# A bidirectional scan kernel: the neighbour chunk's state as an extra column of the data, and sums of a layer's last chunk from an accumulator

## The chip, the cores and the metric

One core of one Trainium2 chip. The metric is device microseconds of the whole kernel; the median of three runs before the change is 5370.0 us (5369.94 to 5373.72).

## What is computed

The input is 16 images of 192 channels and 56 x 56 = 3136 positions. Three layers of one kind and one of another follow each other, each adding to x what it computes from a group norm of x.

A layer of the first kind (RWKV's WKV, in both directions) makes k, v and r by 192 x 192 products, and runs along the 3136 positions, forward and backward, with a fixed decay per channel:

```python
no = jnp.maximum(o, u + kt)
A = jnp.exp(o - no)
Bw = jnp.exp(u + kt - no)
y = (A * p + Bw * vt) / (A * q + Bw)
```

The state p is a decayed sum of exp(k) v, q one of exp(k). The mean of the forward and the backward y is multiplied by sigmoid(r), normalised over the channels, multiplied by Wo and added to x. The last layer takes the maximum of x at neighbours two rows and two columns away (cyclic), concatenates x and that maximum less x, and applies a 1 x 1 convolution, batch norm and GELU.

## The kernel before

Two images are one pair: 2 x 192 channels are three rows (`j`) of 128 partitions, rows 0 and 2 the first 128 channels of either image, row 1 the other 64 of both. A pair's 3136 positions are 7 chunks of L = 448. There are 8 pairs, in two streams of four. Each pair goes through the runs of three WKV layers and one convolution layer; between layers its chunks lie in DRAM.

**Slots.** All chunk-sized data live in 33 slots of SBUF, `Slot` (L501). A slot holds three rows of L + 2 columns; `t` is columns 0 to L - 1, `full` all of them. Column L of an x chunk takes the group mean (`mean_column`, L750), so that the products deliver their own bias. Slots are handed out first in, first out.

**A forward unit (A)** of a chunk: keys (`a_keys`, `a_exp`: ek = exp(k)), values (`a_values`; for the last chunk it also writes the mean column, since the gate product will read it), q scan over ek (`a_q`), `a_save`, bonus (`a_den`), inversion by Ln and Exp on ScalarE, ekv = v ek (`a_ekv`), p scan over ekv (`a_p`), its `save`, bonus (`a_num`), product on POOL (`a_y`).

**A backward unit (B)** runs from the last chunk to the first: gate (`b_gate`, `b_exp`), q and p scans in reverse (`b_q`, `b_p`), `b_den`, `b_num`, mixing on POOL (`b_mix`), squares and their channel sums (`b_squares`, `b_sums`), deviation (`b_rs1` to `b_rs3`), spreading it by TensorE (`b_spread`), `b_scale`, output product (`b_out`), residual (`b_x`), statistics for the next layer's group norm (`b_stats`, by `chunk_stats` on ScalarE). **A convolution unit (C)** is `c_rows`, `c_columns`, `c_product`, `c_end`; beside its chunk it loads a ring, the two strips of the neighbour chunks, by two DMAs on SP (L813, L814).

**The scan** (L836) is one VectorE instruction per row. The decay comes from PSUM, the state of the neighbour chunk by `save` (L841): a copy of the last column of the three rows into a small carry tile, which the scan takes as its initial value. The q carry is copied on ScalarE, the p carry on POOL or VectorE. The first chunk of a direction has the constant 0.0.

**The bonus** (L849) is one VectorE instruction on rows 0 and 2 and one on row 1, in place.

**The order** on every engine is written out by hand. Steps pair a B unit of one stream with an A or C unit of the other. There are 102 steps with B and A (`both_a`, `both_a_first`), 42 with B and C (`both_c`), 66 with A alone (`forward_a`), 14 with C alone (`forward_c`), 24 with B alone (`backward_alone`). After a layer's B chunk 0 the other stream's last A unit runs alone: there `forward_a` holds the late parts `l` of that B chunk, from `b_rs2` to `b_x` and the statistics. With the sums complete, `norm_sums` (L728), `norm_var` and `norm_fold` make the next layer's norm; `gap()` places one of these parts where one is pending.

The waits between instructions are not written by hand. They are put in when the program is built, from the stretches of the tiles that each instruction reads and writes.

```python
self.full = keep.tile([P, 3, L + 2], F32, tag=self.tag, name=name(what))
self.t = self.full[:, :, 0:L]
...
init = 0.0 if first else run.carry[key][:, j, :]
V.tensor_tensor_scan(
    s.t[:, j, order], dec[:, column(j)].to_broadcast([P, L]), data.t[:, j, order], init, ALU.mult, ALU.add
)
```

Of the kernel before, what the change touches and what calls it, by code (L numbers as in the profile page):

```python
# [473 lines left out]
def fast_path(ctx: ExitStack, tc: tile.TileContext, flag, x, wproj, wfold, wcfold, wconst, wgroup, sums, picks, vecs, out):  # L474
# [26 lines left out]
    class Slot:  # L501
        def __init__(self, what):
            self.tag = free.pop(0)
            self.full = keep.tile([P, 3, L + 2], F32, tag=self.tag, name=name(what))
            self.t = self.full[:, :, 0:L]
# [25 lines left out]
    def column(j):  # L531
        return slice(j % 2, j % 2 + 1)
# [172 lines left out]
    class Run:  # L705
        def __init__(self, pr, l, stats, src=None, first=None):
            self.pr, self.l, self.stats, self.src = pr, l, stats, src
            self.xa, self.xb, self.xz = {}, {}, {}
            if first is not None:
                self.xa[0] = first  # L710
            self.begun = False
            self.bias, self.carry, self.ps = {}, {}, {}
            self.ek, self.ekv, self.h, self.den, self.sg, self.rs = {}, {}, {}, {}, {}, {}
            self.m, self.ml, self.q, self.p = {}, {}, {}, {}
# [3 lines left out]

    def chunk_stats(stats, xt, c):

        for j in ORDER:
            S.activation(junk, xt[:, j, :], AF.Identity, accum_out=stats[:, 0, j, c : c + 1])  # L722
            S.activation(junk, xt[:, j, :], AF.Square, accum_out=stats[:, 1, j, c : c + 1])  # L723
# [106 lines left out]

    def scan(run, key, data, order, first, last):
        dec = params[run.l][0]
        s = Slot(key)
        for j in ORDER:
            init = 0.0 if first else run.carry[key][:, j, :]
            V.tensor_tensor_scan(  # L836
                s.t[:, j, order], dec[:, column(j)].to_broadcast([P, L]), data.t[:, j, order], init, ALU.mult, ALU.add
            )
        return s

    def save(run, key, s, col, eng=G):  # L841

        run.carry[key] = stile("c" + key)
        if key == "q":
            S.activation(run.carry[key], s.t[:, :, col : col + 1], AF.Copy)  # L845
        else:
            eng.tensor_copy(run.carry[key], s.t[:, :, col : col + 1])  # L847

# [4 lines left out]

    AHEAD, BACK = slice(0, L, 1), slice(None, None, -1)


    def a_keys(run, c):
        product(run, "k", run.w[0], run.xa[c], c == 0)
        run.ek[c] = Slot("ek")
        if c == 0:  # L860
            take_bias(run, "k", S)
# [17 lines left out]
    def a_ekv(run, c):  # L879
        if c == 0:  # L880
            take_bias(run, "v", V)
        e, ps, b = Slot("ekv"), run.ps["v"], run.bias["v"]
        run.ekv[c] = e
        for j in ORDER:
            V.scalar_tensor_tensor(e.t[:, j, :], ps[j][:, 0:L], b[:, j, :], run.ek[c].t[:, j, :], ALU.add, ALU.mult)  # L885
            release(ps[j])

    def a_q(run, c):
        run.den[c] = scan(run, "q", run.ek[c], AHEAD, c == 0, c == NL - 1)

    def a_save(run, c):
        save(run, "q", run.den[c], L - 1)

    def a_p(run, c, eng=G):
        run.h[c] = scan(run, "p", run.ekv[c], AHEAD, c == 0, c == NL - 1)
        if c < NL - 1:
            save(run, "p", run.h[c], L - 1, eng)

# [12 lines left out]
    def a_y(run, c):  # L911
# [3 lines left out]
        if c in (0, NL - 1):  # L915
# [4 lines left out]
            if c == NL - 1:  # L920
                G.tensor_mul(chk[:, 0], run.carry["q"], grow)

# [21 lines left out]
    def b_q(run, c):  # L944
        if c not in run.q:
            run.q[c] = scan(run, "q", run.ek[c], BACK, c == NL - 1, c == 0)
            if c > 0:
                save(run, "q", run.q[c], 0)

# [5 lines left out]
    def b_p(run, c):  # L955
        if c not in run.p:
            run.p[c] = scan(run, "p", run.ekv[c], BACK, c == NL - 1, c == 0)
            if c > 0:
                save(run, "p", run.p[c], 0)

# [62 lines left out]
    def b_x(run, c):  # L1023
        wob, ps, xs = params[run.l][4], run.ps["o"], run.xb[c]
        for j in ORDER:
            xj = xs.t[:, j, :]
            V.scalar_tensor_tensor(xj, ps[j][:, 0:L], wob[:, column(j)], xj, ALU.add, ALU.add)  # L1027
            release(ps[j])
        nc.sync.dma_start(run.dst[c], xs.t)

    def b_stats(run, c):
        xs = run.xb.pop(c)
        chunk_stats(run.new, xs.t, c)
        if c == 0:
# [331 lines left out]
    def forward_a(a, nback, nfront):  # L1366
# [10 lines left out]
        if l and late[l] == 0:  # L1377
            squares_and_sums(l)
            b_rs1(*l)
            late[l] = 0.5  # L1380
        if l and late[l] == 0.5:
            b_rs2(*l)
            b_rs3(*l)
            late[l] = 1
        if l:
            b_spread(*l)
        elif ahead:
            keys(nfront)
        store()
        a_q(*a)  # L1390
        a_save(*a)
        if ahead and not l:
            exp_keys(nfront)
        a_den(*a)
        gap()
        invert(den())
        a_ekv(*a)
        gap()
        if l:
            b_scale(*l)  # L1400
            if ahead:
                keys(nfront)
                exp_keys(nfront)
            b_out(*l)
            late[l] = 2
        sum_up()
        if nback is not None:
            b_gate(*nback[1:])
        a_p(*a)
        gap()  # L1410
        if l:
            add(l)
            sum_up()
        a_num(*a)
        a_y(*a)
# [237 lines left out]
```

## Time and profile before

| | |
|---|---|
| median of the runs | 5370.0 us |
| profiled execution | 5382.8 us |
| its span | 5381.0 us |
| VectorE busy | 5014.9 us (93%) |
| TensorE busy | 4629.7 us (86%) |
| ScalarE busy | 3681.2 us (68%) |
| GpSimd (POOL) busy | 2770.3 us (51%) |
| mean granted TensorE clock | 0.916 |

A row of the groups names the line, the engine, the operation, what it writes and reads, partitions x elements, and the count; then the busy time and the mean length of one, then the engine's idle time ahead of them and what ended most of it. Lengths of neighbours on VectorE overlap by some 0.08 us, so that a mean length is a little above busy time over count. In a timeline a row is a start, a length, engine, line and tiles; equal neighbours are merged (x3). DVE is VectorE, ACT ScalarE, PE TensorE, SPq the queue that issues most DMAs.

### The profile page before, as it was taken

Reading aid. Unit: us, or ns where it says so; the run is one execution under the profiler, and the core shown is the slowest. Engines: PE = TensorE matmul, PEld = TensorE weight load, DVE = VectorE, ACT = ScalarE, POOL = GpSimd, SP = SyncE. Lnnn points to the kernel's source line nnn. Section 1 sums busy time; section 2 is a strip of 40 time slices with the busy share of each in tenths; the row PEclk is TensorE's granted clock in tenths of the full one; section 3 lists DMA queues with packets and bytes.
Section 4 is the critical chain, followed back from the end, with each engine's and each line's share of the span. In section 5 each row is a group of like instructions: output and inputs, shape, how many; then the busy total and the mean of one; then the engine's idle time right before and its main releaser. Section 6 shows DMA issues by size and latency. Waiting matters only on the chain. (4 is left out here: it accounts for less than half of the span.)

```text
span 5381.0 us, 50984 instructions
## 1 busy us (share of the span) xinstructions
PE 4629.7 (86%) x15206; PEld 1498.6 (28%) x15206; DVE 5014.9 (93%) x6556; ACT 3681.2 (68%) x7035; POOL 2770.3 (51%) x2164
## 2 busy tenths in 40 slices
PE   6888988989798898888979888888888988898897
PEld 2222322223232222222323222222222222222222
DVE  6989999999999999999999999999999999999996
ACT  6777667767676676676667767667667566676673
POOL 1555555645454465555444455555535455555463
PEclk8989989989899898998989989999898998999898
DMA  5222212124243212213425121221343312222233
GB/s 149 78 80 72 85 66 88 63 90 140 87 131 89 82 63 73 74 67 105 144 87 150 56 74 67 85 74 62 111 139 94 111 56 74 70 77 80 77 102 115
DMA packets 314271, 482.42 MB, mean 90 GB/s; under 512 B 66432, under 2 KB 306688, under 8 KB 313984
## 3 DMA queue, kind: packets, MB, share of 16 engines
q1 hardware_dynamic: 312832, 477.59, 27.9%
q8 instruction: 123, 2.02, 0.2%
q10 hardware_dynamic: 1152, 1.48, 0.1%
q14 instruction: 164, 1.34, 0.1%
HBM read 324.83 MB, written 154.14 MB: 89 GB/s over the span
## 5 line engine op out<-in xcount | busy, mean ns | idle before, releaser
L913 POOL TENSOR_TENSOR p<-p,q 128x1344 f32<-128x1344 f32 x168 | 510.1, 3037 | 887.8 <-ACT q L909 472.1
L969 POOL TENSOR_TENSOR ekv<-ekv,ek 128x448 f32<-128x448 f32 x504 | 618.2, 1227 | 677.1 <-DVE p L1014 304.9
L836 DVE TENSOR_TENSOR_SCAN p<-fdecays,cp,ekv 128x448 f32<-128x448 f32 x864 | 928.5, 1130 | 7.2 <-POOL p L913 4.5
L836 DVE TENSOR_TENSOR_SCAN q<-fdecays,cq,ek 128x448 f32<-128x448 f32 x864 | 929.2, 1131 | 1.9 <-PE st L987 0.2
L971 POOL TENSOR_TENSOR p<-p,sg 128x448 f32<-128x448 f32 x504 | 599.4, 1189 | 54.5 <-ACT cq L845 10.7
L970 POOL TENSOR_TENSOR p<-p,ekv 128x448 f32<-128x448 f32 x504 | 600.6, 1192 | 39.5
L847 POOL COPY cp<-p 128x3 f32<-128x3 f32 x271 | 196.4, 725 | 686.9 <-DVE p L836 454.3
L978 ACT ACTIVATE ek<-p 128x448 f32<-128x448 f32 x504 | 283.6, 573 | 259.4 <-POOL p L971 257.5
L591 PE MATMUL ops<-p,fwo 128*128 128x448 f32 x336 | 223.5, 755 | 275.3 <-DVE p L1014 275.2
L866 ACT ACTIVATE ek<-k,k 128x448 f32<-128x448 f32 x504 | 292.1, 630 | 243.0 <-PE k L594 216.4
L723 ACT ACTIVATE fjunk<-x 128x448 f32<-128x448 f32 x672 | 387.6, 577 | 21.1
L722 ACT ACTIVATE fjunk<-x 128x448 f32<-128x448 f32 x672 | 384.6, 572 | 14.6
L851 DVE SCALAR_TENSOR_TENSOR q<-ek,fcc,q 128x896 f32<-128x896 f32 x336 | 337.1, 1043 | 51.1 <-ACT cq L845 51.1
L1009 PE MATMUL rsb<-rs,fpicks 32*128 32x448 f32 (+1 forms) x1008 | 335.8, 594 | 48.8 <-ACT rs L1003 46.7
L1027 DVE SCALAR_TENSOR_TENSOR x<-ops,fwob,x 128x448 f32<-128x448 f32 x504 | 315.9, 674 | 52.2 <-PE ops L594 27.1
L851 DVE SCALAR_TENSOR_TENSOR ek<-ek,fcc,q 128x896 f32<-128x896 f32 x336 | 361.6, 1117 | 2.8 <-POOL chk L919 2.8
L851 DVE SCALAR_TENSOR_TENSOR ekv<-ekv,fcc,p 128x896 f32<-128x896 f32 x336 | 330.4, 1024 | 1.2
L934 ACT ACTIVATE sg<-r,r 128x448 f32<-128x448 f32 x504 | 311.9, 624 | 15.8 <-PE r L594 10.4
L885 DVE SCALAR_TENSOR_TENSOR ekv<-v,v,ek 128x448 f32<-128x448 f32 x504 | 312.9, 677 | 0.0
L1014 DVE TENSOR_TENSOR p<-p,rsb 128x448 f32<-128x448 f32 x504 | 281.5, 614 | 31.1 <-PE rsb L1009 31.0
L851 DVE SCALAR_TENSOR_TENSOR p<-ekv,fcc,p 128x896 f32<-128x896 f32 x336 | 293.4, 913 | 10.0 <-POOL cp L847 9.7
L906 ACT ACTIVATE q<-q 128x1344 f32<-128x1344 f32 x168 | 222.4, 1324 | 90.4 <-DVE q L851 65.9
(232 smaller groups left out, 11795.3 us busy)
## 6 DMA issues: line engine op xcount, KB each, us to landing
x<-xd SPq DMA_DIRECT2D x240, 672.0 KB, 5.5
xd<-x SPq DMA_DIRECT2D x168, 672.0 KB, 4.0
x<-in_x_dram SPq DMA_DIRECT2D x320, 224.0 KB, 4.6
x<-in_x_dram SPq DMA_DIRECT2D x320, 112.0 KB, 4.6
out_dram<-ml SPq DMA_DIRECT2D x112, 224.0 KB, 2.3
ring<-xd SPq DMA_DIRECT2D x112, 168.0 KB, 5.3
wkv<-in_wfold_dram SPq DMA_DIRECT2D x24, 640.0 KB, 5.5
out_dram<-ml SPq DMA_DIRECT2D x112, 112.0 KB, 2.3
```

The source lines that it names most:

```text
L722: S.activation(junk, xt[:, j, :], AF.Identity, accum_out=stats[:, 0, j, c : c + 1])
L723: S.activation(junk, xt[:, j, :], AF.Square, accum_out=stats[:, 1, j, c : c + 1])
L836: V.tensor_tensor_scan(s.t[:, j, order], dec[:, column(j)].to_broadcast([P, L]), data.t[:, j, order], init, ALU.mult, ALU.add)
L851: by_channel(lambda js, i: V.scalar_tensor_tensor(dst.t[:, js, :], e.t[:, js, :], cc[:, i : i + 1], state.t[:, js, :], ALU.mult, ALU.add))
L885: V.scalar_tensor_tensor(e.t[:, j, :], ps[j][:, 0:L], b[:, j, :], run.ek[c].t[:, j, :], ALU.add, ALU.mult)
L913: G.tensor_mul(run.h[c].t, run.h[c].t, den.t)
L934: S.activation(sg.t[:, j, :], ps[j][:, 0:L], AF.Exp, bias=b[:, j, :], scale=-1.0, accum_out=run.chk[:, at : at + 1])
L969: G.tensor_mul(y.t[:, j, :], y.t[:, j, :], den.t[:, j, :])
L970: G.tensor_add(h.t[:, j, :], h.t[:, j, :], y.t[:, j, :])
L971: G.tensor_mul(h.t[:, j, :], h.t[:, j, :], sg.t[:, j, :])
L1009: PE.matmul(ps[j][:, :L], pick[rows, j, :], rs[rows, :], start=True, stop=True)
L1027: V.scalar_tensor_tensor(xj, ps[j][:, 0:L], wob[:, column(j)], xj, ALU.add, ALU.add)
```

## The change

A slot becomes one flat stretch of 3 (L + 2) + 2 columns, seen as three rows. `full` begins at column 2 of it; `lead` begins one column earlier, so that it has a column ahead of column 0. `save` copies the last state into the neighbour chunk's data: forward into the column ahead of the next chunk's ek or ekv, backward into column L of the previous chunk's. A scan that isn't a direction's first runs over L + 1 columns from the constant 0.0, and reads the state as its first element. For this the next chunk's ek and ekv slots are taken at the save if they don't exist yet (`slot_of`). The q save stays on ScalarE.

The residual of chunk 0, a layer's last, writes its row sums by an accumulator output of VectorE; ScalarE then forms only the squares of that chunk.

`forward_a` with late parts gets an order of its own: the q scan ahead of `b_rs2`, the output product ahead of the gate and of the keys, the bonus `a_num` ahead of the residual, and no `gap()`.

```diff
-            self.full = keep.tile([P, 3, L + 2], F32, tag=self.tag, name=name(what))
+            flat = keep.tile([P, 3 * (L + 2) + 2], F32, tag=self.tag, name=name(what))
+            rows = lambda at: flat[:, at : at + 3 * (L + 2)].rearrange("p (j n) -> p j n", j=3)[:, :, 0 : L + 1]
+            self.full, self.lead = rows(2), rows(1)
             self.t = self.full[:, :, 0:L]
...
-    def chunk_stats(stats, xt, c):
+    def chunk_stats(stats, xt, c, whole=False):
         for j in ORDER:
-            S.activation(junk, xt[:, j, :], AF.Identity, accum_out=stats[:, 0, j, c : c + 1])
+            if not whole:
+                S.activation(junk, xt[:, j, :], AF.Identity, accum_out=stats[:, 0, j, c : c + 1])
             S.activation(junk, xt[:, j, :], AF.Square, accum_out=stats[:, 1, j, c : c + 1])
...
-    def scan(run, key, data, order, first, last):
+    def scan(run, key, data, step, first):
         dec = params[run.l][0]
         s = Slot(key)
         for j in ORDER:
-            init = 0.0 if first else run.carry[key][:, j, :]
+            if first:
+                out, e = s.t[:, j, ::step], data.t[:, j, ::step]
+            elif step > 0:
+                out, e = s.lead[:, j, :], data.lead[:, j, :]
+            else:
+                out, e = s.full[:, j, ::-1], data.full[:, j, ::-1]
             V.tensor_tensor_scan(
-                s.t[:, j, order], dec[:, column(j)].to_broadcast([P, L]), data.t[:, j, order], init, ALU.mult, ALU.add
+                out, dec[:, column(j)].to_broadcast([P, L if first else L + 1]), e, 0.0, ALU.mult, ALU.add
             )
         return s
-    def save(run, key, s, col, eng=G):
-        run.carry[key] = stile("c" + key)
-        if key == "q":
-            S.activation(run.carry[key], s.t[:, :, col : col + 1], AF.Copy)
+    def save(s, step, to, eng=G):
+        src, dst = (s.t[:, :, L - 1 : L], to.lead[:, :, 0:1]) if step > 0 else (s.t[:, :, 0:1], to.full[:, :, L : L + 1])
+        if eng is S:
+            S.activation(dst, src, AF.Copy)
         else:
-            eng.tensor_copy(run.carry[key], s.t[:, :, col : col + 1])
+            eng.tensor_copy(dst, src)
...
+    def slot_of(slots, c, what):
+        if c not in slots:
+            slots[c] = Slot(what)
+        return slots[c]
...
     def a_p(run, c, eng=G):
-        run.h[c] = scan(run, "p", run.ekv[c], AHEAD, c == 0, c == NL - 1)
+        run.h[c] = scan(run, "p", run.ekv[c], AHEAD, c == 0)
         if c < NL - 1:
-            save(run, "p", run.h[c], L - 1, eng)
+            save(run.h[c], AHEAD, slot_of(run.ekv, c + 1, "ekv"), eng)
...
-            V.scalar_tensor_tensor(xj, ps[j][:, 0:L], wob[:, column(j)], xj, ALU.add, ALU.add)
+            V.scalar_tensor_tensor(
+                xj, ps[j][:, 0:L], wob[:, column(j)], xj, ALU.add, ALU.add,
+                accum_out=run.new[:, 0, j, c : c + 1] if c == 0 else None,
+            )
...
         xs = run.xb.pop(c)
-        chunk_stats(run.new, xs.t, c)
+        chunk_stats(run.new, xs.t, c, c == 0)
...
         if l:
+            if late[l] == 0.5:
+                b_rs2(*l)
+                b_rs3(*l)
+            b_spread(*l)
+            a_den(*a)
+            invert(den())
+            sum_up()
+            a_ekv(*a)
             b_scale(*l)
+            b_out(*l)
+            if nback is not None:
+                b_gate(*nback[1:])
             if ahead:
                 keys(nfront)
                 exp_keys(nfront)
-            b_out(*l)
-            late[l] = 2
...
+            a_p(*a)
+            a_num(*a)
             add(l)
             sum_up()
-        a_num(*a)
```

More of the change, by code (lines that the diff above doesn't have):

```diff
@@ L711, in __init__ @@
             self.begun = False
-            self.bias, self.carry, self.ps = {}, {}, {}
+            self.bias, self.ps = {}, {}
             self.ek, self.ekv, self.h, self.den, self.sg, self.rs = {}, {}, {}, {}, {}, {}
@@ L852, in bonus @@
             dst.t[:, js, :], e.t[:, js, :], cc[:, i : i + 1], state.t[:, js, :], ALU.mult, ALU.add))
-    AHEAD, BACK = slice(0, L, 1), slice(None, None, -1)
+    AHEAD, BACK = 1, -1
+    def slot_of(slots, c, what):
+        if c not in slots:
+            slots[c] = Slot(what)
+        return slots[c]
     def a_keys(run, c):
         product(run, "k", run.w[0], run.xa[c], c == 0)
-        run.ek[c] = Slot("ek")
+        slot_of(run.ek, c, "ek")
         if c == 0:
@@ L881, in a_ekv @@
             take_bias(run, "v", V)
-        e, ps, b = Slot("ekv"), run.ps["v"], run.bias["v"]
-        run.ekv[c] = e
+        e, ps, b = slot_of(run.ekv, c, "ekv"), run.ps["v"], run.bias["v"]
         for j in ORDER:
@@ L888, in a_q @@
     def a_q(run, c):
-        run.den[c] = scan(run, "q", run.ek[c], AHEAD, c == 0, c == NL - 1)
+        run.den[c] = scan(run, "q", run.ek[c], AHEAD, c == 0)
     def a_save(run, c):
-        save(run, "q", run.den[c], L - 1)
+        if c < NL - 1:
+            save(run.den[c], AHEAD, slot_of(run.ek, c + 1, "ek"), S)
+        else:
+            run.last = stile("cq")
+            S.activation(run.last, run.den[c].t[:, :, L - 1 : L], AF.Copy)
     def a_p(run, c, eng=G):
-        run.h[c] = scan(run, "p", run.ekv[c], AHEAD, c == 0, c == NL - 1)
+        run.h[c] = scan(run, "p", run.ekv[c], AHEAD, c == 0)
         if c < NL - 1:
-            save(run, "p", run.h[c], L - 1, eng)
+            save(run.h[c], AHEAD, slot_of(run.ekv, c + 1, "ekv"), eng)
     def a_den(run, c):
@@ L920, in a_y @@
             if c == NL - 1:
-                G.tensor_mul(chk[:, 0], run.carry["q"], grow)
+                G.tensor_mul(chk[:, 0], run.last, grow)
     def b_gate(run, c):
@@ L945, in b_q @@
         if c not in run.q:
-            run.q[c] = scan(run, "q", run.ek[c], BACK, c == NL - 1, c == 0)
+            run.q[c] = scan(run, "q", run.ek[c], BACK, c == NL - 1)
             if c > 0:
-                save(run, "q", run.q[c], 0)
+                save(run.q[c], BACK, run.ek[c - 1], S)
     def b_den(run, c):
@@ L956, in b_p @@
         if c not in run.p:
-            run.p[c] = scan(run, "p", run.ekv[c], BACK, c == NL - 1, c == 0)
+            run.p[c] = scan(run, "p", run.ekv[c], BACK, c == NL - 1)
             if c > 0:
-                save(run, "p", run.p[c], 0)
+                save(run.p[c], BACK, run.ekv[c - 1])
     def b_num(run, c):
@@ L1380, in forward_a @@
             late[l] = 0.5
[L1381 to L1387, printed above, removed]
+        if not l and ahead:
             keys(nfront)
@@ L1391, in forward_a @@
         a_save(*a)
[L1392 to L1398, printed above, removed]
-        if l:
+        if l:
+            if late[l] == 0.5:
[6 more added lines that the diff above has]
+            a_ekv(*a)
             b_scale(*l)
+            b_out(*l)
+            if nback is not None:
+                b_gate(*nback[1:])
             if ahead:
@@ L1403, in forward_a @@
                 exp_keys(nfront)
-            b_out(*l)
-            late[l] = 2
[L1406 to L1411, printed above, removed]
+            a_p(*a)
+            a_num(*a)
             add(l)
             sum_up()
-        a_num(*a)
+        else:
+            if ahead:
+                exp_keys(nfront)
+            a_den(*a)
+            gap()
+            invert(den())
+            a_ekv(*a)
+            gap()
+            sum_up()
+            if nback is not None:
+                b_gate(*nback[1:])
+            a_p(*a)
+            gap()
+            a_num(*a)
         a_y(*a)
```

## The prediction

> **What bounds the kernel now.** I read the page's busy shares first, then the groups by line with shapes kept apart, then the timeline of a layer end, then that of the tail.
>
> ```profile
> PE 4629.7 (86%) x15206; PEld 1498.6 (28%) x15206; DVE 5014.9 (93%) x6556; ACT 3681.2 (68%) x7035; POOL 2770.3 (51%) x2164
> ...
> L836 DVE TENSOR_TENSOR_SCAN q<-fdecays,cq,ek 128x448 f32<-128x448 f32 x864 | 929.2, 1131 | 1.9 <-PE st L987 0.2
> L836 DVE TENSOR_TENSOR_SCAN p<-fdecays,cp,ekv 128x448 f32<-128x448 f32 x864 | 928.5, 1130 | 7.2 <-POOL p L913 4.5
> ...
> L836 DVE TENSOR_TENSOR_SCAN q<-fdecays,ek 128x448 f32<-128x448 f32 x144 | 146.3, 1071 | 6.7 <-ACT ek L866 6.0
> L836 DVE TENSOR_TENSOR_SCAN p<-fdecays,ekv 128x448 f32<-128x448 f32 x144 | 146.1, 1070 | 0.0
> ```
>
> VectorE is the bound: 5014.9 of 5381.0 us, in order, and inside the paired steps it has almost no idle time. So microseconds of VectorE are microseconds of the kernel, except where it waits. The last two rows are the form that the change gives to all scans: no carry operand, initial value 0.0. It costs 1071 ns against 1131 ns.
>
> The largest repeated wait is at a layer end: VectorE's timeline, then ScalarE's and TensorE's in the same place (start, length, engine, line, idle time before).
>
> ```profile
> 2045.73 0.15 DVE L751 COPY x<-nm 128x3 f32<-128x3 f32 x1
> 2045.92 0.63 DVE L997 TENSOR_TENSOR rs<-st,rs 64x448 f32<-64x448 f32 x1
> 2046.58 3.23 DVE L836 TENSOR_TENSOR_SCAN q<-fdecays,cq,ek 128x448 f32<-128x448 f32 x3
> 2050.08 2.18 DVE L851 SCALAR_TENSOR_TENSOR q<-ek,fcc,q 128x896 f32<-128x896 f32 x2 [0.27 <-ACT cq L845]
> ...
> 2070.00 0.20 DVE L728 TENSOR_REDUCE mv<-stats 128x6 f32<-128x42 f32 x1 [3.17 <-ACT fjunk L723]
> ...
> 2065.80 0.58 ACT L722 ACTIVATE fjunk<-x 128x448 f32<-128x448 f32 x1
> ...
> 2048.22 0.54 PE L599 MATMUL v<-x,wkv 128*64 128x448 f32 x1
> ```
>
> The reduction L728 waits 3.17 us for six statistics that ScalarE works off from 2065.80 to 2069.97, 0.70 us each. There are 17 such ends; the row of L728 has 77.5 us of waits, 20.6 of it the start's. The last line matters below: the value product of that step ends on TensorE at 2048.76, 3 us after L751 has run.
>
> The tail is VectorE and SP, one convolution chunk after another:
>
> ```profile
> 5294.48 0.50 DVE L1051 TENSOR_TENSOR m<-ring,x 128x336 f32<-128x336 f32 x1
> 5294.89 0.85 DVE L1052 TENSOR_TENSOR m<-x 128x672 f32<-128x672 f32 x1
> ...
> 5298.22 1.56 DVE L1066 TENSOR_TENSOR ml<-ml,x 128x1344 f32<-128x1344 f32 x1
> 5299.81 1.56 DVE L1067 TENSOR_TENSOR m<-m,ml 128x1344 f32<-128x1344 f32 x1
> ...
> 5335.01 1.61 DVE L1051 TENSOR_TENSOR m<-ring,x 128x336 f32<-128x336 f32 x1 [2.58 <-DMA ring<-xd]
> ...
> 5330.25 0.59 SPq L813 DMA_DIRECT2D ring<-xd  x1
> 5330.88 0.62 SPq L814 DMA_DIRECT2D ring<-xd  x1
> ```
>
> L1052 needs nothing of L1051 and starts 0.09 us before its end. L1067 reads what L1066 writes and starts 0.03 us after its end. A VectorE instruction that must wait for the one just before it therefore costs 0.12 us more (117 ns in the trace's records: L1066 and L1067 start 34 ns after, unbound neighbours 83 ns before the end).
>
> [...]
>
> **The change part by part.**
>
> *Scans.* 1728 (864 + 864) lose 60 ns and gain one column: 1728 x 0.058 = -100 us. The carries are copied by the same engines at the same places. A group of three (0.17 us) gives nothing where VectorE then waits for TensorE anyway: L1027 waits 73 times, L1014 31, several of them in one step. For some 45 lost groups: +8.
>
> *What the flat tile does to the waits.* A slot was a three-dimensional tile; now it is a flat one, seen through a rearranged view. I built the changed program and compared the waits that it writes with those before. An access to rows 0 and 2 is now ordered against row 1, and a column of all three rows against the rows. The diff names none of this.
>
> (a) Each bonus is two instructions, rows 0 and 2, then row 1. The second now waits for the first: 4 x 168 = 672. With some that now wait for the scan just ahead, 708 bonus instructions wait for their predecessor; before, none. So do L1052 and L1053: 112. 820 x 0.117 = +96 us, less 4 for those inside waits that remain. On ScalarE 138 exponentials wait for the save just ahead; it is idle a third of the time, so nothing.
>
> (b) L751 (mean_column in a_values) writes column L of a chunk whose columns 0 to L-1 the value product is reading. It now waits for the product's last matmul. In the timeline above that is from 2045.73 to 2048.8, and over the 17 layer ends 3.0 to 4.1 us, mean 3.5. Behind it on VectorE stand the scan q, L997, the bonus, ekv and L1014, whose result TensorE needs for the output product, and behind that the gate product and the statistics.
>
> (c) A ring has two DMAs into disjoint columns (L813, L814). The second now waits for the first to land, about 4 us, and SP's later loads and stores stand behind it. In the paired steps the rings land over 20 us early, so nothing. In the tail three chunks have no margin (L1051 at 5335, 5344 and 5354): 3 x 4 = +12.
>
> *Earlier slots.* The next chunk's ekv slot is taken at the save, one step early. Every last user had finished over 2 us before the save's present place, so the saves wait for nothing new. Loads behind L971 wait 1.5 us on SP, far ahead of need. In the first forward and backward pass slots are short: three q scans would stand 3.7 to 6.3 us behind the POOL product L913, where p scans now stand 2.5 and 2.0. Bounds 0 and +16; I take +8.
>
> *Layer ends.* Three of six statistics go: 3 x 0.70 = -2.1 us on the path that ends at L728. The three others still start when TensorE's gate product has given ScalarE its bias, as now. L997 behind the scan removes the 0.27 us wait and, with the shorter scan, saves 0.5. So one end moves by 3.5 - 0.5 - 2.1 = +0.9; 17 of them +15. L1027's waits there (0.56, 0.59) are covered by the bonus put ahead, but the chain through TensorE is longer, so this gains nothing.
>
> *Accumulators.* 72 L1027 write a sum. Unknown: 0 to 0.6 us each (nothing, or the instruction again). 51 are covered by the wait at L728, which otherwise would lengthen VectorE's path by up to 1.8 us per end; I take +1, and up to +13.
>
> *The other order in forward_a.* In six ends beside a convolution the output product goes ahead of the keys and L1027 no longer waits 2.2 us. But there ScalarE's 18 statistics end the wait (2.91 us before the bonus); three are gone, and the exponential of the keys comes 2 us later in their place. Nothing.
>
> Sum: -100 + 8 + 96 - 4 + 12 + 8 + 15 + 1 = +36 us on the profiled execution (5382.8, span 5381.0). It lies 12.8 above the median of the runs, 5370.0; I add the same 36: 5406 us.
>
> **Rivals.** *The layer end wins, faster.* Place: L751 against the value product. If TensorE is through with that product when L751 comes, the 3.5 us go and each end gains about 2.6: 36 - 17 x 3.5 = -24, 5346 us. The sum changes sign where the wait is below 1.4 us. For: TensorE ran ops at half pace at 2054, so a shift could land in a better stretch of its clock. Against: the product follows the norm's sums on TensorE, and these follow POOL, which the change does not hasten.
>
> *The waits cost nothing.* Then it is the diff as it reads: -100 + 8 - 2.1 x 17 = 5242. Against: L1066 and L1067, each 56 times.
>
> *All cancels.* The waits at the ends fall half as long, and the tail's DMAs overlap otherwise: 5365 to 5380.
>
> *SP becomes the bound.* The ring's stall at each of 56 chunks pushes stores, and these free slots: 1 us at half the steps is 120 us, 5490. Against: over 20 us of margin.
>
> **How the numbers follow.** The forecast has 0.60, the layer end's rival 0.12, nothing-costs 0.05, all-cancels 0.17, SP 0.06. 0.2% is about what can be told from no change here, 11 us: faster 0.16, same 0.19, slower 0.65. The forecast's own range is 5383 to 5445: ends +-1 us (17), start 8, accumulators 12, lost overlap 10. To hold 8 in 10 it takes in all-cancels and the edge of the first rival: 5354 to 5450.
>
> **What would show it.** Scans at 1073 ns. The second bonus, L1052 and L1053 starting 0.03 us after their predecessor. A 3 to 4 us wait of L751 for TensorE's v, and L728's wait under 3.17. L814 about 4 us behind L813. VectorE's busy sum down by some 100, its idle time up by more. I am wrong if the bonus pairs still overlap, or if L751 doesn't wait.

## The result, and the profile after

| | before | after |
|---|---|---|
| median of the runs, same chip | 5371.9 us | 5461.6 us |
| profiled execution | 5382.8 us | 5459.2 us |
| its span | 5381.0 us | 5457.3 us |
| VectorE busy | 5014.9 us | 5028.0 us |
| VectorE idle in its span | 366 us | 429 us |
| scans, both forms of each | 2150.1 us | 2048.2 us |

The changed kernel is slower: the ratio is 1.0166 (95% interval 1.0149 to 1.0184). 5406 us was forecast, 5354 to 5450 the range; the time lies outside it. Slower was right, its size was not. The spans differ by 76.3 us where I had +36.

The busy shares of the page after, the answer to the first line of the prediction:

```profile
PE 4665.8 (85%) x15206; PEld 1502.5 (28%) x15206; DVE 5028.0 (92%) x6628; ACT 3640.3 (67%) x6891; POOL 2769.3 (51%) x2164
```

The scans gave 102 us of VectorE's time, and yet its busy sum rose: other instructions became longer. The groups by line after, with shapes kept apart (busy time, mean ns, idle time before and what ended it):

```profile
L845 DVE TENSOR_TENSOR_SCAN q<-fdecays,ek 128x449 f32<-128x449 f32 x864 | 878.3, 1071 | 16.1 <-POOL p L930 13.7 <-ACT ek L880 1.3
L845 DVE TENSOR_TENSOR_SCAN p<-fdecays,ekv 128x449 f32<-128x449 f32 x864 | 877.5, 1070 | 4.3 <-POOL p L930 1.6
...
L1014 DVE TENSOR_TENSOR rs<-st,rs 64x448 f32<-64x448 f32 x168 | 105.4, 627 | 46.4 <-ACT rs L1010 41.7
...
L754 DVE COPY x<-nm 128x3 f32<-128x3 f32 x56 | 39.5, 705 | 55.4 <-PE v L602 54.7 <-DMA x<-in_x_dram 0.4 <-DMA xd<-x 0.3
...
L731 DVE TENSOR_REDUCE mv<-stats 128x6 f32<-128x42 f32 x32 | 6.2, 192 | 35.4 <-ACT fjunk L726 35.4
```

The scans take 1071 and 1070 ns (1073 forecast, 2 ns of it assumed for one more column, which no run had shown); before, 448 columns without a carry operand took the same 1071 and 1070, so the added column doesn't show. L754 (L751 before) waits 54.7 us for the value product, as forecast (17 x 3.5 = 60). But its own length, without the wait, grew from 161 to 705 ns in the mean of all 56. L731's wait fell from 77.5 to 35.4 us. L1014 (L997 before) now waits 41.7 us for ScalarE where it waited 14.2: the prediction has no such term.

The same layer end as in the prediction, before, VectorE's range check and POOL's product:

```profile
2061.80 0.18 DVE L632 TENSOR_TENSOR req<-chk,flimit 128x33 f32<-128x33 f32 x1
...
2047.68 3.04 POOL L913 TENSOR_TENSOR p<-p,q 128x1344 f32<-128x1344 f32 x1 [4.08 <-ACT q L909]
```

The copy L751 stood 2 us ahead of that product then (2045.73). After, VectorE and POOL (start, length, idle time before):

```profile
2074.78 1.92 DVE L754 COPY x<-nm 128x3 f32<-128x3 f32 x1 [2.71 <-PE v L602]
...
2092.58 1.51 DVE L634 TENSOR_TENSOR req<-chk,flimit 128x33 f32<-128x33 f32 x1
...
2097.82 0.20 DVE L731 TENSOR_REDUCE mv<-stats 128x6 f32<-128x42 f32 x1 [0.54 <-ACT fjunk L726]
...
2125.55 0.63 DVE L1014 TENSOR_TENSOR rs<-st,rs 64x448 f32<-64x448 f32 x1 [2.80 <-ACT rs L1010]
...
2073.65 3.03 POOL L930 TENSOR_TENSOR p<-p,q 128x1344 f32<-128x1344 f32 x1 [4.04 <-ACT q L926]
2091.00 3.04 POOL L930 TENSOR_TENSOR p<-p,q 128x1344 f32<-128x1344 f32 x1 [14.32 <-DVE p L860]
```

After its wait of 2.71 us the copy of 128 x 3 numbers takes 1.92 us, and ends at 2076.70, just when POOL's product ends (2073.65 + 3.03 = 2076.68). L634, a comparison of 128 x 33 numbers, does the same: 1.51 us, for 0.18 before, beside POOL's product until 2094.04. What makes the two long there these rows don't show. The wait moved the copy in time, to where POOL was busy. The check was moved there by the other order in `forward_a`, not by the wait: below, it takes 0.19 us in e4 (flat tile, old order) and 1.38 us in e1 (no such wait, new order).

The tail after: SP's two ring loads, and VectorE's wait for one of them:

```profile
5387.53 0.64 SPq L816 DMA_DIRECT2D ring<-xd  x1
5392.22 0.52 SPq L817 DMA_DIRECT2D ring<-xd  x1
...
5411.80 0.51 DVE L1071 TENSOR_TENSOR m<-ring,x 128x336 f32<-128x336 f32 x1 [4.75 <-DMA ring<-xd]
```

The second load is issued 4.7 us after the first (0.63 before), as forecast. But from the sixth-last convolution chunk to the end it is 76.9 us (5380.4 to 5457.3), for 74.8 before (5306.2 to 5381.0): +2, not +12.

### The profile page after: what moved, and what is told of

It is laid out like the page before. It is cut to its first block, busy times and chain, and to the rows that moved or that the text cites. A ratio compares the mean times of both kernels' runs of the same rounds, so it can differ in the third digit from the quotient of the medians.

```text
span 5457.3 us, 51046 instructions
## 1 busy us (share of the span) xinstructions
PE 4665.8 (85%) x15206; PEld 1502.5 (28%) x15206; DVE 5028.0 (92%) x6628; ACT 3640.3 (67%) x6891; POOL 2769.3 (51%) x2164
## 3 DMA queue, kind: packets, MB, share of 16 engines
q14 instruction: 165, 1.35, 0.1%
## 5 line engine op out<-in xcount | busy, mean ns | idle before, releaser
L845 DVE TENSOR_TENSOR_SCAN q<-fdecays,ek 128x449 f32<-128x449 f32 (+1 forms) x1008 | 1024.6, 1071 | 23.8 <-POOL p L930 13.7
L845 DVE TENSOR_TENSOR_SCAN p<-fdecays,ekv 128x449 f32<-128x449 f32 (+1 forms) x1008 | 1023.6, 1070 | 4.3 <-POOL p L930 1.6
L856 POOL COPY ekv<-p 128x3 f32<-128x3 f32 x271 | 188.3, 695 | 734.8 <-DVE p L845 385.7
L1026 PE MATMUL rsb<-rs,fpicks 32*128 32x448 f32 (+1 forms) x1008 | 370.7, 649 | 166.8 <-ACT rs L1020 166.8
L860 DVE SCALAR_TENSOR_TENSOR q<-ek,fcc,q 128x896 f32<-128x896 f32 x336 | 348.6, 1038 | 60.4 <-ACT ek L854 52.0
L726 ACT ACTIVATE fjunk<-x 128x448 f32<-128x448 f32 x672 | 387.5, 577 | 20.4
L725 ACT ACTIVATE fjunk<-x 128x448 f32<-128x448 f32 x600 | 343.1, 572 | 12.9
L860 DVE SCALAR_TENSOR_TENSOR p<-ekv,fcc,p 128x896 f32<-128x896 f32 x336 | 308.6, 919 | 20.4 <-POOL ekv L856 13.6
L951 ACT ACTIVATE sg<-r,r 128x448 f32<-128x448 f32 x504 | 312.2, 625 | 19.0 <-PE r L596 13.4
L923 ACT ACTIVATE ek<-ek 128x1344 f32<-128x1344 f32 x168 | 221.1, 1316 | 71.6 <-DVE ek L860 71.6
```

The lines of the kernel that those rows point to most:

```text
L845: V.tensor_tensor_scan(out, dec[:, column(j)].to_broadcast([P, L if first else L + 1]), e, 0.0, ALU.mult, ALU.add)
L860: by_channel(lambda js, i: V.scalar_tensor_tensor(dst.t[:, js, :], e.t[:, js, :], cc[:, i : i + 1], state.t[:, js, :], ALU.mult, ALU.add))
L1026: PE.matmul(ps[j][:, :L], pick[rows, j, :], rs[rows, :], start=True, stop=True)
```

## The experiments

Theory 1 was the prediction's: the flat tile's coarser order of accesses costs what was lost, and without it the scans keep their 92 us and each layer end its 2.1 us. Theory 2: another part of the change (the other order of `forward_a`, or the scans themselves) costs as well or brings less. From the fifth run on the question was where the scans' gain goes. Times are medians; "before" ran beside each group, at 5376 to 5382 us.

### The four parts, taken apart

**e1_rows: all of the change, but a slot of three dimensions.** Accesses to different rows are then not ordered against each other.

```diff
-            flat = keep.tile([P, 3 * (L + 2) + 2], F32, tag=self.tag, name=name(what))
...
+            wide = keep.tile([P, 3, L + 2], F32, tag=self.tag, name=name(what))
+            self.full, self.lead = wide[:, :, 1 : L + 2], wide[:, :, 0 : L + 1]
```

> The whole change, but with the slot as a tile of three dimensions, three rows of L + 2 columns, in which t is columns 1 to L, lead begins at column 0 and full ends at column L + 1. Theory 1 (the flat tile's coarser ordering costs what was lost: self-waits of the bonus pairs and of the convolution's maxima, about 92 us, the mean column's wait for the value product, and what follows from it at the 17 layer ends): the second bonus instruction starts 0.08 us before the end of the first again, the mean column does not wait, the time is 5372 - 100 (scans) + 8 - 17 x 2.6 (layer ends) = about 5236, between 5220 and 5290. Theory 2 (forward_a's other order, or statistics and scans brought next to POOL's product, cost the larger part of the unforeseen 55 us): the waits go, but the layer ends keep their long copies and the wait for the deviation; 5462 - 92 - 12 = about 5358, 5330 to 5390.

Measured: 5323.4 us, 0.9894 of before (0.9878 to 0.9911). The waits are gone (the mean column's is 0.0 us, for 54.7), the kernel is faster than before, but 87 us slower than theory 1 wants.

**e2_flat: the kernel before with the flat slot alone.**

```diff
-            self.full = keep.tile([P, 3, L + 2], F32, tag=self.tag, name=name(what))
+            flat = keep.tile([P, 3 * (L + 2) + 2], F32, tag=self.tag, name=name(what))
+            self.full = flat[:, 2 : 2 + 3 * (L + 2)].rearrange("p (j n) -> p j n", j=3)[:, :, 0 : L + 1]
```

> The kernel before, with the flat slot alone: carries, scans, statistics and orders as before. Theory 1: self-waits +92, the tail's second ring load +12, the mean column at 17 layer ends 3.5 us each, of which the wait for the statistics takes up none: +60, and the start +8 or less: 5372 + 165 = about 5537, between 5500 and 5570. If that wait is covered at the layer ends, about 5476. Theory 2 (the tile costs little, the other parts cost): under 5450.

Measured: 5509.2 us, 1.0238 (1.0221 to 1.0255): the tile alone costs 129 us. The groups by line of this run:

```profile
L752 DVE COPY x<-nm 128x3 f32<-128x3 f32 x56 | 38.9, 695 | 53.6 <-PE v L601 53.5
...
L729 DVE TENSOR_REDUCE mv<-stats 128x6 f32<-128x42 f32 x32 | 6.2, 193 | 71.0 <-ACT fjunk L724 71.0
```

The mean column costs its wait of 53.5 us and 30 us of length; only 6.5 us come back at the wait for the statistics and 5 at the one for the norm's sums behind it. For the self-waits I take VectorE's time from the end of each instruction's predecessor to its own end, longer waits apart. The four bonuses need 41 us more in sum than before (p forward 22, ekv 17, ek 10, q -8), where 708 x 0.117 = 83 were forecast; the convolution's maxima 3 us more, where 13 were. So p and ekv lose their 0.12 us per pair. The second half of the q bonus costs its 20 us too, but the first half gets 23 us shorter: in the 85 paired steps `both_a` it takes 1.24 us, for 1.36 before, because VectorE comes to it 0.12 us later and stands less long beside POOL's product there.

**e3_rows_old_order and e4_flat_old_order: forward_a in its old order**, once with the slot of three dimensions, once with the flat one. The edit puts back the lines of `forward_a` from before.

> As the run with the three-dimensional slot and the whole change, but forward_a in its old order. Theory 1: the other order is worth little, within 20 us of that run (0.5 to 1 us at each of 17 ends by the scan put ahead of the deviation). Theory 2: the other order is what hurts the layer ends, so this one is faster than that run by 30 us or more.

> The changed kernel with its flat slot, but forward_a in its old order. Theory 1 (the mean column's wait for the value product is what delays each end, whatever the order behind it): 5462 within 25 us. Theory 2 (the other order moved VectorE's small instructions onto POOL's product): 5462 - 60 = about 5400.

Measured: 5303.4 us, 0.9856 (0.9840 to 0.9872), and 5440.2 us, 1.0111 (1.0094 to 1.0128). The other order costs 20 us on either tile. Its wait of b_x for the output product falls (48 to 11 us in the slot of three dimensions), but the check of 128 x 33 gets 29 us longer, and the q bonus of `forward_a` 21 us (8 in length, 13 in waits), now that it stands behind the deviation.

**e6_scans and e7_accumulators: each alone.** e6 is e3 with all statistics on ScalarE; e7 is before with the accumulators.

```diff
...
-            V.scalar_tensor_tensor(xj, ps[j][:, 0:L], wob[:, column(j)], xj, ALU.add, ALU.add)
+            V.scalar_tensor_tensor(
+                xj, ps[j][:, 0:L], wob[:, column(j)], xj, ALU.add, ALU.add,
+                accum_out=run.new[:, 0, j, c : c + 1] if c == 0 else None,
+            )
```

> The three-dimensional slot, the wide scans and the saves into the data alone: statistics all on ScalarE, forward_a in its old order. Theory (each of 1728 scans saves 58 ns and keeps it, apart from some 17 us at the start): 5380 - 100 + 17 = about 5297. If the accumulators of the run with both (5303) were worth their 2.1 us at each of 17 ends, this one is about 5340.

> The kernel before with the sums of a layer's last chunk from accumulators, and nothing else. Theory (what is saved at the wait for the statistics, 2.2 us at each of 17 ends, is given back at the next wait for the deviation, which grew from 0.84 to 2.80 us in the run with the scans): 5380 - 38 - 14 + 28 + some = 5355 to 5380. Rival (the gain is kept, and the longer wait for the deviation comes from the shorter scans): 5380 - 45 = about 5335.

Measured: 5365.2 us, 0.9967 (0.9955 to 0.9980), and 5335.7 us, 0.9912 (0.9895 to 0.9928). Both theories failed; e7 came out at its rival's number. The accumulators keep their gain, 47 us. The scans, which take 100 us less on VectorE here too, bring 17. I had blamed the accumulators for losing what the scans lose.

### Where the scans' gain goes

The same accounting, e6 against before: scans -100 us. Against it: q bonus +30, wait for the deviation (L1013, L997 before) +28, q scans that wait at the start +15, wait of b_scale for the spread +9, and smaller ones. The first two are the larger part.

The q bonus in the paired step `both_a`. Before (VectorE, then POOL):

```profile
470.55 3.23 DVE L836 TENSOR_TENSOR_SCAN p<-fdecays,cp,ekv 128x448 f32<-128x448 f32 x3
473.69 1.37 DVE L851 SCALAR_TENSOR_TENSOR q<-ek,fcc,q 128x896 f32<-128x896 f32 x1
...
472.98 1.13 POOL L971 TENSOR_TENSOR p<-p,sg 128x448 f32<-128x448 f32 x1
474.05 1.05 POOL L847 COPY cp<-p 128x3 f32<-128x3 f32 x1
```

And the same place in e6:

```profile
472.78 3.05 DVE L844 TENSOR_TENSOR_SCAN p<-fdecays,ekv 128x449 f32<-128x449 f32 x3
475.75 1.75 DVE L859 SCALAR_TENSOR_TENSOR q<-ek,fcc,q 128x896 f32<-128x896 f32 x1
...
475.42 1.13 POOL L987 TENSOR_TENSOR p<-p,sg 128x448 f32<-128x448 f32 x1
476.49 1.05 POOL L855 COPY ekv<-p 128x3 f32<-128x3 f32 x1
```

The first bonus instruction begins 0.42 us before POOL's last mixing product ends (474.11) in the one, 0.80 us before (476.55) in the other. It is as much longer, 1.75 for 1.37 us, and ends 0.95 us behind POOL in both. Two stretches run side by side here, from the end of VectorE's ek bonus (460.70 in the one, 463.11 in the other) on. One is ScalarE's inversion, 2.8 us, and POOL's nine mixing products, 10.6 us: 13.4 us in both runs. The other is VectorE's ekv bonus, b_scale, ekv, q scan, b_x and p scan: 13.0 us before, 12.6 in e6. VectorE was ahead already, and its shorter scans only make it stand longer: 6 of a step's 12 scans, 0.35 us a step, in 85 steps 30 us. A steady step went from 25.3 to 25.0 us, where 12 scans are 0.70.

The wait for the deviation stands in `both_a_first`. Before (POOL, ScalarE, VectorE):

```profile
2086.91 1.13 POOL L971 TENSOR_TENSOR p<-p,sg 128x448 f32<-128x448 f32 x1
...
2088.08 0.58 ACT L978 ACTIVATE ek<-p 128x448 f32<-128x448 f32 x1 [2.49 <-POOL p L971]
...
2096.79 0.63 DVE L997 TENSOR_TENSOR rs<-st,rs 64x448 f32<-64x448 f32 x1 [0.84 <-ACT rs L993]
```

And in e3:

```profile
2058.58 2.07 POOL L987 TENSOR_TENSOR p<-p,sg 128x448 f32<-128x448 f32 x1
...
2060.68 0.58 ACT L994 ACTIVATE ek<-p 128x448 f32<-128x448 f32 x1 [2.13 <-POOL p L987]
...
2069.41 0.63 DVE L1013 TENSOR_TENSOR rs<-st,rs 64x448 f32<-64x448 f32 x1 [2.80 <-ACT rs L1009]
```

Counted from the layer's norm (its rstd), VectorE's bonus ek (L851, L859) comes 0.35 us earlier now, and this product is stretched from 1.13 to 2.07 us; before, the bonus stretched the product behind it, to 1.99 us (at 2088.00). ScalarE's square waits for this one, and so ScalarE's work of some 8 us up to the first square of the deviation comes 0.9 us later, while VectorE arrives 1 us earlier. 0.84 us of wait became 2.80, at 14 of 17 layer ends. This is read from the traces; no run takes the stretching of this product away and changes nothing else.

**e8_scan_first: work for VectorE in that wait** (e3, and `a_q` ahead of `b_rs2` in `both_a_first`).

```diff
         b_sums(*l)
-        deviation(l)
+        b_rs1(*l)
         a_q(*a)
+        b_rs2(*l)
+        b_rs3(*l)
+        late[l] = 1
```

> The run with the three-dimensional slot and the old forward_a (5303), with one edit: in the first paired step of a layer (both_a_first) the forward q scan stands ahead of the subtraction L1013 on VectorE, not behind it. Theory (VectorE stands still for 2.80 us at 13 such steps and 0.84 at 4, for ScalarE's square of the sums, while three scans of 3.0 us with all operands ready stand behind): nearly all of the 40 us goes, 5303 - 38 = about 5265. Rival (the deviation, and with it the output product and the residual, come late instead): 5290 to 5310.

Measured: 5304.8 us, 0.9857 of before, no change from e3 (5303.4, 0.9856), and in the rival's range. The groups by line in e3, then in e8:

```profile
L1030 DVE TENSOR_TENSOR p<-p,rsb 128x448 f32<-128x448 f32 x504 | 281.2, 613 | 34.7 <-PE rsb L1025 34.7
L1013 DVE TENSOR_TENSOR rs<-st,rs 64x448 f32<-64x448 f32 x168 | 105.4, 627 | 46.9 <-ACT rs L1009 42.2
```

```profile
L1030 DVE TENSOR_TENSOR p<-p,rsb 128x448 f32<-128x448 f32 x504 | 281.2, 613 | 78.2 <-PE rsb L1025 78.0
L1013 DVE TENSOR_TENSOR rs<-st,rs 64x448 f32<-64x448 f32 x168 | 105.4, 628 | 6.1 <-ACT rs L1009 1.0
```

41 us left one wait and 43 came to the next. So this stretch of a layer's first step waits for the chain POOL, ScalarE, TensorE, and moving VectorE's scans into the wait gains nothing.

**e12_sigmoid_first: that chain shortened** (e10 below, and ScalarE's sigmoid in the time in which it waited for POOL).

```diff
-        b_squares(*l, (0, 2))
-        b_q(*b)
+        b_squares(*l, (0,))
         b_sigmoid(*b)
+        b_q(*b)
+        b_squares(*l, (2,))
```

> The run with b_x between p scan and q bonus, with one more edit in both_a_first: on ScalarE the sigmoid stands ahead of the square of row 2, which waits 2.1 to 2.5 us for POOL's mixing product. Theory (that idle time on ScalarE is what makes the deviation's first square late): the wait of VectorE for it falls from 2.80 to about 1.9 us (then the sums on TensorE decide), 15 us less than the run without this edit. Rival (POOL's last mixing product sets the sums): within 5 us of it.

Measured: 5287.4 us, 0.9828 (0.9811 to 0.9844), 16 us less than e10. The wait for the deviation fell from 42.0 to 31.9 us, as expected. It is the fastest of the kernels that compute the whole result: 1.7% faster than before, and 3.3% faster than the change as it came (0.9828 / 1.0166).

**e10_add_between and e13_acc_add_between: b_x between p scan and q bonus**, on e3 and on e7.

```diff
-        if l:
-            add(l)
...
         a_p(*a)
         gap()
+        if l:
+            add(l)
         a_den(*a)
```

> The run with the three-dimensional slot and the old forward_a (5303), with one edit in the paired step both_a: the residual b_x, which reads PSUM, stands between the p scan and the q bonus, not ahead of the p scan. Theory (the first q bonus instruction, which starts during POOL's last mixing product, stands still[...]: 1.66 us in 85 places against 0.67 where POOL is idle): some 70 of the 85 lose about 1.0 us, 5303 - 70 = about 5235. Rival (POOL's product is only late in the same step, and VectorE waits elsewhere for the same chain): 5295 to 5310.

> The kernel before with the accumulators (5336), and with b_x between p scan and q bonus, scans and carries as before. Theory (the shorter scans' gain was spent in the collision with POOL's mixing product): here the collision is 0.68 us in some 70 places, so 5336 - 45 = about 5290, and the run with the same order and the short scans is 55 to 65 us faster than this one, where it was 32 us faster without this edit. Rival (the scans' gain goes elsewhere): the two differ by 32 us again.

Measured: 5303.4 and 5333.8 us, no effect in either, and the bonus no shorter (1.74 us in e10, 1.66 in e3). The edit was idle: b_x and the p scan both stood ahead of the bonus already, and in either order it starts at the same time. These two runs decide nothing. The expectations, those of e14, e18 and e19 too, also carry a wrong length: 0.67 us is the bonus of one row; the first instruction has two rows and takes 1.14 us alone, so that 0.5 us were to be had in each place, not 1.0.

**e14_next_scan and e16_acc_next_scan: three scans more ahead of the bonus**, on e3 and on e7.

```diff
         gap()
+        if nback is not None:
+            b_q(*nback[1:])
         a_den(*a)
```

> The run with the three-dimensional slot and the old forward_a (5303), with one edit in both_a: the next step's backward q scan (3 us, operands ready, decay from PSUM) stands ahead of the q bonus, not behind the step. Theory (POOL's last mixing product and its copy, which end 0.78 and 1.79 us after the bonus's present start, cost it 1.0 us in some 70 places): the bonus falls from 1.66 to about 0.70 us, POOL's copy from 1.05 to 0.19; of 70 us some 20 come back at the bonuses ek, which move towards POOL's product of the forward unit: about 5250, between 5230 and 5275. Rival (another chain sets the step): above 5290.

> The kernel before with the accumulators (5336), long scans and carries, and the edit of both_a alone: the next backward q scan ahead of the q bonus. Theory (the short scans' gain went into the collision at the bonus): there the collision is 0.68 us, so the edit brings 28 us less than on the short scans, and short scans are worth 60 us with it (32 without). Rival (the scans' gain goes elsewhere): they are worth 32 again.

Measured: 5322.5 and 5350.2 us. The q bonus lost its stall as expected (42 us less in e14), and the time rose by 19 and 15 us. In e14 29 us came back at the ek bonus, which now meets POOL's product of the forward unit, 15 at b_scale, 11 at the p scan, 8 each at the q scans and at the maxima. The short scans are worth 28 us in this order, 32 without: the rival's number. Moving the instruction away from one product moved the next onto another.

**e15_bonus_later and e17_both: the bonuses of both_a_first behind the forward q scan and ekv**, and row 1's square, the gate and the channel sums ahead of them; both on e12, e17 with e14's edit in place of e10's.

```diff
         b_p(*b)
+        a_q(*a)
+        a_ekv(*a)
...
         b_den(*b)
...
-        a_ekv(*a)
...
-        deviation(l)
-        a_q(*a)
```

> The run with the sigmoid first (5287), with both_a_first in another order: forward q scan and ekv, which read PSUM, stand ahead of the two bonuses, which now run 2.60 and 3.52 us a pair beside POOL's mixing products, where a pair takes 1.74 alone; the square of the deviation stands behind the inversion on ScalarE, ahead of the gate's exponentials. Theory (bonuses and mixing products hold each other up): 2.6 us less on VectorE in each of 17 steps, POOL's products back at 1.14 us, the wait for the deviation not over 1.9: 5287 - 40 = about 5247. Rival (the chain POOL, ScalarE, TensorE to the deviation is as long without stretched products): 5275 or more.

> Both edits on the sigmoid-first run: next backward q scan ahead of the q bonus in both_a, and both_a_first with forward scan and ekv ahead of the bonuses. Theory: the gains add: 5287 - 50 - 40 = about 5200, between 5180 and 5230. Rival: not under 5260.

Measured: 5323.7 and 5347.6 us, slower than e12 by 36 and 60. Both lie in their rivals' ranges. In e15 the bonuses ek and ekv got shorter by 48 us in sum, as expected. The wait of b_scale grew by 63 us (34.7 to 97.4), since the deviation and its spread came later, and the p save on VectorE by 13.

**e18_short_no_add and e19_long_no_add: POOL's chain itself shortened**, with short scans (e3) and long ones (e7). Both kernels leave the backward y out of the result; they are there to measure POOL's part.

```diff
             G.tensor_mul(y.t[:, j, :], y.t[:, j, :], den.t[:, j, :])
-            G.tensor_add(h.t[:, j, :], h.t[:, j, :], y.t[:, j, :])
             G.tensor_mul(h.t[:, j, :], h.t[:, j, :], sg.t[:, j, :])
```

> The run with the three-dimensional slot, short scans and the old forward_a (5303), without the addition in b_mix: POOL has 6 products per chunk and not 9, 3.6 us less, and the forward and backward y are not added (the backward y is left out of the result). Theory (POOL's mixing chain takes up the short scans' gain): the first q bonus instruction falls from 1.66 to 0.7 us, the wait for the deviation from 2.80 to under 1, and this run is 70 to 95 us faster than the same with long scans. Rival (the gain is lost elsewhere): about 32 us faster, as with the addition.

> The kernel before with the accumulators (5336), long scans and carries, without the addition in b_mix (again the backward y is left out of the result). Theory: the q bonus falls from 1.35 to 0.7 us in 85 places, the wait for the deviation (0.84) goes: 5336 - 55 - 14 = about 5267. Rival: within 20 us of 5336.

Measured: 5139.1 and 5208.8 us, 164 us less than e3 and 127 less than e7. The short scans are worth 69.7 us here, the lower edge of what was expected, and 32.2 with the additions. The first q bonus instruction takes 1.14 and 1.13 us, where it took 1.66 and 1.35. A steady paired step of e18 (VectorE, then POOL):

```profile
648.98 1.73 DVE L859 SCALAR_TENSOR_TENSOR q<-ek,fcc,q 128x896 f32<-128x896 f32 x2
...
644.02 1.17 POOL L986 TENSOR_TENSOR p<-p,sg 128x448 f32<-128x448 f32 x1
```

POOL's last mixing product ends 3.8 us ahead of the bonus. The median step goes from 25.25 us (e19) to 24.38 (e18), where it went from 25.33 (e7) to 25.00 (e3): with POOL out of the way a step keeps the whole of its 0.70 us and more. So POOL's mixing products take up more than half of what was missing: of the 68 us between 32 and the 100 of VectorE's, 37 came back. The edit shortens POOL's chain and takes products away from beside VectorE at once; which of the two counts for how much it can't tell. Of the 30 us still missing, 17 are the q scans' waits at the start. Not as expected: the wait for the deviation did not go but grew, to 57 and 47 us; of it I only know that a shorter POOL chain isn't its cure.

### Two instructions beside POOL's product

**e5_flat_late_mean: the mean column later** (the changed kernel with its flat tile; the copy stands just ahead of the gate product).

```diff
             run.xb[c] = xs
-            mean_column(run, xs)
...
     def b_gate(run, c):
+        if c == NL - 1:
+            mean_column(run, run.xb[c])
```

> The changed kernel with its flat slot and its order, with one edit: the mean column of a layer's last chunk is written just ahead of the gate product that reads it, behind b_scale on VectorE, not just behind the value product. Theory (the column's wait of 2.7 to 4.1 us at 17 ends, and the copy that then stands 1.9 us behind POOL's product, are on VectorE's path): its wait of 55 us and its 33 us of extra length go, 5462 - 88 = about 5375. Rival (a layer end is bound by the chain through TensorE and ScalarE, so the same time comes back at the wait for the statistics): 5440 or more.

Measured: 5399.7 us, 1.0032 (1.0020 to 1.0045), for 1.0166: 1.3% of the time, some 72 us. Wait and length of the copy fell by 87 us in sum, and the q bonus of the same step took 33 us of it, 29 in length: it moved to POOL's product in the copy's place (1.15 us for its first instruction at the 17 layer ends with the copy ahead, 2.68 without).

**e11_checks_psum: the check's tiles in PSUM** (e1, whose new order has the long check).

```diff
-    ok = const.tile([P, NCHK], F32, tag="ok", name="fok")
...
-    limit = const.tile([P, NCHK], F32, tag="limit", name="flimit")
+    held = psconst.tile([P, 2 * NLAYERS + 2 * NCHK], F32, tag="decays", name="fdecays")
...
+    ok, limit = held[:, 2 * NLAYERS : 2 * NLAYERS + NCHK], held[:, 2 * NLAYERS + NCHK : 2 * NLAYERS + 2 * NCHK]
```

> The run with the three-dimensional slot and forward_a's new order (5323), with one edit: the two small tiles of the range checks (the limits and the result) lie in PSUM, so that neither check instruction reads two operands from SBUF. Theory (in the new order the check of 128 x 33 stands 1.0 us longer behind POOL's product[...]): it falls from 1.43 to about 0.2 us at the layer ends, and the time to 5323 - 28 = about 5295. Rival ([...]the wait for the statistics takes the time up): 5315 to 5325.

Measured: 5325.0 us, no gain on e1's 5323.4. The groups by line:

```profile
L730 DVE TENSOR_REDUCE mv<-stats 128x6 f32<-128x42 f32 x32 | 6.1, 192 | 59.9 <-ACT fjunk L725 59.9
L634 DVE TENSOR_TENSOR req<-chk,fdecays 128x33 f32<-128x33 f32 (+1 forms) x32 | 5.7, 179 | 0.2
```

The check fell from 1075 to 179 ns in the mean (34.4 to 5.7 us): with one operand in PSUM it doesn't stand behind POOL, although POOL's product still runs on both sides of it in 23 of 24 places. So what made this check long is that both of its operands lay in SBUF; no other instruction was tried this way. But the wait for the statistics rose from 40.1 to 59.9 us, and that of q scans by 10: the check had only filled a wait. What makes the statistics 1.2 us later in the new order than in e3 (39.1 us of wait) was not tried.

## Why the prediction was wrong, by its own steps

The spans of four runs and the two kernels form a ladder on which each step of the sum can be measured alone. Before has 5381.0 us.

| step | forecast | measured | spans |
|---|---|---|---|
| scans -100, lost overlap +8, start +8 | -84 | -20 | e6 5361.4 |
| statistics -2.1 x 17, accumulators +1 | -35 | -60 | e3 5301.3 |
| flat tile: +96 - 4, +12, 3.5 x 17 | +164 | +136 | e4 5437.7 |
| other order, -0.5 x 17 | -9 | +20 | after 5457.3 |
| sum | +36 | +76 | |

**What failed first is the opening sentence**, that microseconds of VectorE are microseconds of the kernel, and with it the term 1728 x 0.058. The size of a scan is right to 3 ns (1071 and 1070, for 1073). Its worth isn't: VectorE is 93% busy, but part of its busy time is standing behind POOL. A bonus counts as busy while it stands there, and the view shows no idle time. Of the 65 us missing in this step, 30 are at the q bonus and 28 at the wait for the deviation. The start cost 15 for my 8 (inside my bounds of 0 and 16); b_scale's wait took 9, about the 8 that I had for lost groups. I had priced 45 lost groups where VectorE waits; I had not looked for what ends beside an instruction that is long without a wait. The first bonus instruction's 1362 ns in these 85 places, where one alone takes 1140, stood in the trace of before. That the gain goes to POOL's mixing products is shown for more than half of it (e18 against e19); for the wait for the deviation, which e18 did not bring down, it is argued.

**Statistics and accumulators.** 60 us instead of 35; e7 alone has 47. I had held that the three squares still start when TensorE has given ScalarE its bias, and counted 2.1 us at L728 alone. That wait falls by 42 us in e7, as counted (36); another 15 us fall at L735's wait for the norm's sums (26.4 to 11.1 us), which I had not counted. With the short scans the step is worth 13 us more: b_x's wait for the output product grew by 17 us in e7 (52.2 to 69.9) and not from e6 to e3 (49.5 to 48.0). Why was not tried. The accumulators are nearly free: 72 reads of 83 ns, 6 us, and the instructions are no longer than before (673 ns in the mean, for 674).

**Flat tile.** The self-waits exist as forecast: the second bonus starts 35 ns after the first, not 83 ns before its end, and L1072 and L1073 likewise. But of +96 they cost about 44 (41 + 3), since a VectorE that comes later stands less long beside POOL's products (in e2 the first half of the q bonus takes 1.24 us, for 1.36). The mean column costs more than its wait of 54 us: another 30 us in length, on POOL's product. I had asked what stands behind L751 on VectorE, not what runs beside it after 3 us. The ring's second load is 4.7 us late, as forecast, and costs 2 us, not 12: of the three chunks without margin the first waits 2.2 us longer than before (4.75 for 2.58), the second no longer at all (0 for 0.97), the third 1.1 us longer (2.18 for 1.09).

**Other order.** -0.5 us at each end was the scan ahead of L997; it didn't come. The order costs 1.2 us at each end, the wait for the statistics being that much longer when the check's stall is taken away (e11).

**Rivals.** The first one needed L751's wait to go; it stayed (54.7 us), and e5 shows 72 us for the wait and the long copy together. That the waits cost nothing, and all else follows the diff, would have been 5242; even without these waits e3 has 5303. SP did not become the bound. The forecast of VectorE's busy sum (down by 100) was wrong by the same cause as the scans: it rose by 13.

**Luck in the sum.** The steps miss by +64, -25, -28 and +29 us, and partly cancel; that "slower" came out right rests on the flat tile's term, the largest. Nor are the steps independent: the first q bonus instruction takes 1.66 us in e3 and 1.51 in the changed kernel, whose self-waits bring VectorE to it later.

## What to carry to other kernels

Before pricing a shorter instruction, look at what runs on the other engines at its end: if two engines start a stretch together and take equally long, a gain on one is a longer stall at the meeting point (here 13.4 us of ScalarE and POOL beside 13.0, then 12.6, of VectorE), and VectorE's stall behind POOL's product hides in the busy time, where only an instruction much longer than its shortest form betrays it (1.75 us for 1.14). Moving the stalled instruction moved another one there (33 of 87 us in e5, 29 of 42 in e14); shortening the other engine's chain is what freed the gain here (e18: 69.7 us for the short scans, 32.2 with the additions). And give a tile as many dimensions as its parts are used apart: here one dimension less cost 129 us, and the same idea on three dimensions is faster than the kernel before.

## What the runs showed of the hardware

- A copy of 128 x 3 numbers took 1.91 to 2.20 us beside POOL's product, 0.16 alone (changed kernel); a comparison of 128 x 33 took 1.51 us (changed kernel), and 0.18 again in the mean once one operand lay in PSUM (e11). It works both ways: POOL's product of 448 columns took 1.13 us alone and 2.07 beside a bonus (e3), POOL's copy of 128 x 3 0.19 and 1.05 (e14).
- The wide forward scans begin at column 1 of the flat slot and at column 0 of e1's; in the mean with the backward ones, scans take 1070 to 1071 ns in both. An initial value that is an operand cost 60 of 1131 ns (before: 1131 with it, 1071 with the constant).
- An accumulator output on VectorE cost a read of 83 ns, 72 times; the instruction itself stayed at 0.67 us (changed kernel: 673 ns in the mean of 504, 674 before).
